# Signs and router steps at written places, exact parts tile by tile, weight sums at the seam, and the last stores on other queues, in an attention and gated feed-forward kernel

## The chip, the cores and the metric

The kernel runs on one core of one Trainium2 chip. TensorE (PE) multiplies matrices into PSUM banks; VectorE (DVE), ScalarE (ACT) and GpSimd (POOL) do elementwise work; SyncE (SP) here only issues transfers, and ACT's and POOL's instruction queues can issue them too. All engines run side by side and wait for each other by semaphores. The metric is the time of one execution on the device in microseconds (us), less being better. The kernel before took 1203.75 us (median of 3 runs, 1203.04 to 1204.23).

## The reference

Everything is float32. The input is 4 sequences of 512 rows of 1024 numbers. With `_layernorm`, a causal attention with 16 heads of 64 and rotary positions, and a feed-forward part whose weight matrix counts only by its signs:

```python
q = (xn @ Wq).reshape(b, s, 16, 64)          # k, v likewise; q and k are rotated
logits = jnp.where(causal, q @ k.T, -1e9) / jnp.sqrt(64)
s = (softmax(logits) @ v).reshape(b, s, 1024) @ Wo

routing = softmax(xn @ gate_w.T)             # 8 experts
in_scale, out_scale = routing @ in_channel_scale, routing @ out_channel_scale
g = silu(xn * in_scale @ sign(weight).T * out_scale + bias)

out = x + s * g
```

## The kernel before

**Stages.** The projections to Q, K and V and the attention run first, as 16 groups: 4 batches `b` by 4 groups `g` of two head pairs. Group k computes its own projections while it does the attention of group k - 1. Then comes a seam, in which the attention of the last group is done beside the first feed-forward products, and then eight pairs of row tiles (`pairs`, index `q`) with feed-forward product, output projection and the final gating.

**Order.** Only TensorE's instructions run in the order in which the program writes them (`manual_schedule(engines={PE})`). The queues of the other engines, SP's transfers too, are ordered by a planner at compile time, in which what is written earlier goes first among what is ready.

**A group.** `project(b, g)` is a generator. It makes three projections (m = 0, 1, 2 for Q, K, V), each as seven products of half-size blocks in the manner of Strassen and Winograd, with sums `S1..S4` of weights (`form_w`, L249) and `T1..T4` of inputs (`form_x`, L261) on VectorE. It yields after every matmul (Q, K) or every second one (V), 28 times a projection, 84 times a group. Each projection takes four PSUM banks one after another from the pool `ring` (4 banks): its products 1 and 2 (L329 to L334), 7 and 6, 5 and 4, and 3. The third bank is freed by the addition at L356, the fourth by the one after product 3 (recorded at L327). The pool is shared with the transposed probabilities (`ptp`), the attention output (`pv`), the transposes of x and the router's three small banks.

The other work of a group is a list of `pieces`. `attention_pieces` makes 16 of them: five transposes of the first unit's probabilities, `scores_1` with `values`, five transposes of the second unit, `scores_3` with `values`, an empty place, `scores_02`, two empty places. `interleave` deals the 84 steps evenly among the pieces. A first transpose (L457) of the next group needs the probabilities of `scores_02`: mask (L402), maximum (L406), exponential on ScalarE (L409), reciprocal (L417) and a multiplication on GpSimd (L419), first for the block of 384 columns, then for that of 128.

**Extras.** In the first group of a batch (`g == 0`) six pieces are spread evenly between the others: the load of two tiles of the weight matrix, `router(b, 0)` (64 matmuls of x with the gate weights `gw`, L495), `make_sign` of the first tile (four VectorE instructions, L573 and L574), `router(b, 1)` (a transpose and the softmax over the experts on VectorE, L506 to L532), `make_sign` of the second tile, and `router(b, 2)` (a transpose, a copy, four small stores). With 22 pieces they stand at places 3, 7, 11, 15, 19 and 21, `scores_3` at 14 and `scores_02` at 17. The very first group has no attention; there the same extras and the load and split of the two scale tables (`split_scales`, L557 to L564) are its only pieces, nine of them. Eight of its 84 steps have been run before it starts.

**The seam.** `load_xn` brings back the normalized rows of pairs 0 and 1 into one tile. `in_scales` multiplies them by the routed scales. `split(q)` makes a part `hi` that float32r holds exactly (ScalarE, L632) and the rest `lo` (VectorE, L633), for both row tiles of a pair into one buffer (pool `hl`, one deep). `ffn` multiplies both by the signs (L821), 16 steps a pair, and VectorE takes the result out of its ring bank (L831). `sum_wo` (L813) makes the sums t1 to t4 of the output weights, four instructions each: t1 and t3 beside pair 0's products, t2 beside pair 1's, t4 written in `project_out(0)`. t1 lies in the place of pair 0's rows, t2 in that of pair 1's; the gate values `Z` of pair 1 lie in a tile shared with t4. `out_scales(1)` (L642, copied by ScalarE at L652) uses the banks of the scores.

**The end.** `project_out(q)` makes the output projection by seven products (L933), `finish` adds and gates them, and GpSimd's queue stores the rows. For the last pair product 3 comes last, with two VectorE steps (L982, L983) and the last store on SP (L984) behind it; the rows of the other tile are stored from GpSimd's queue (L973).

## Time and profile before

| what | value |
|---|---|
| median of the runs shown | 1203.75 us (1203.04 to 1204.23) |
| profiled execution, its own time | 1201.24 us |
| its span | 1199.5 us |
| mean granted TensorE clock | 0.996 of full speed |
| TensorE instructions on the chain that ended last | 89% of the span |
| VectorE on that chain | 7% |
| bytes read and written in HBM | 95.45 MB and 25.43 MB, 101 GB/s over the span |

The span is one execution from the first to the last recorded instruction; the profiled execution's own time holds 1.7 us more. A row of a timeline reads: start, duration, engine, line of the program, operation, output<-input, shape, how many were merged, and in brackets how long the engine had been idle and what ended that. A row of windows reads: the stretch, its length, busy time of PE, PEld (weight loads), DVE, ACT and POOL with the number of instructions in brackets, the granted clock of TensorE, the busy share of the DMA engines and what they moved in GB/s. A float32 matmul is recorded as two instructions, one in float32r as one.

In windows of 20 us over the whole span TensorE is busy for the full 20 us in most of them. The others are 0 to 40, 80 to 100, 260 to 280, 460 to 480, 680 to 700, 840 to 860, 880 to 900 and 1180 to 1200 us.

### The profile page before, as it was taken

What the parts mean: (1) busy time and instruction counts of PE and PEld (TensorE: products, weight loads), DVE (VectorE), ACT (ScalarE), POOL (GpSimd) and SP (SyncE); (2) the same over time, 40 slices, a digit from 0 to 9 for tenths busy, and PEclk for the clock granted to TensorE, in tenths of its full rate; (3) what the DMA queues carried; (4) which work ended last, traced back from release to release, by engine and by line L of the source; (5) the groups of instructions that cost most, each with busy time, mean ns of one, the idle gap of its engine ahead of it and who ended that gap; (6) DMA issues with size and microseconds to landing.
All of it is one profiled execution on the core that took longest, in us unless ns stands there. A gap on an engine that the chain in (4) does not pass through costs nothing.

```text
span 1199.5 us, 17805 instructions
## 1 busy us (share of the span) xinstructions
PE 1170.3 (98%) x6696; PEld 888.1 (74%) x6696; DVE 773.5 (64%) x1395; ACT 492.6 (41%) x1134; POOL 536.3 (45%) x596
## 2 busy tenths in 40 slices
PE   6999999999999999999999999999999999999997
PEld 5988888877878887887888878887764456645663
DVE  6878677776767678576767866666864533453342
ACT  2453655344464644356464534445432121222120
POOL 0464536353443635343353534255355445544543
PEclk9999999999999999999999999999999999999999
DMA  8414323332143232223325212210503523432320
GB/s 299 143 54 136 119 84 109 99 99 80 44 127 111 80 118 94 71 73 115 114 89 185 66 60 80 80 49 19 207 15 138 194 76 105 145 112 68 106 70 36
DMA packets 59814, 122.04 MB, mean 102 GB/s; under 512 B 5200, under 2 KB 40528, under 8 KB 53584
## 3 DMA queue, kind: packets, MB, share of 16 engines
q1 hardware_dynamic: 55008, 111.98, 28.7%
q0 software_dynamic: 4720, 8.92, 2.1%
q8 instruction: 53, 0.87, 0.3%
q14 instruction: 33, 0.27, 0.1%
HBM read 95.45 MB, written 25.43 MB: 101 GB/s over the span
## 4 chain that ended last, share of the span: by engine, by line
PE 89%; DVE 7%; ACT 2%; issue 1%; POOL 0%; DMA 0%; ACTq 0%; DVEq 0%
PE pj L300 32%; PE wo L933 16%; PE pj L308 13%; PE ff L821 9%; PE pv L473 6%; PE sc L391 6%; PE ptp L457 6%; DVE nmx L406 2%; ACT p L409 1%; PE xtp L205 1%; DVE sc L402 1%; PE lg L495 1%; DVE rot L271 1%; DVE S L249 0%; DVE lo L633 0%
## 5 line engine op out<-in xcount | busy, mean ns | idle before, releaser
L419 POOL TENSOR_SCALAR p<-p,rs 128x128 f32<-128x128 f32 (+3 forms) x256 | 169.3, 674 | 204.6 <-DVE rs L417 204.6
L409 ACT ACTIVATE p<-sc,nmx 128x128 f32<-128x128 f32 (+3 forms) x256 | 132.5, 523 | 154.2 <-DVE nmx L406 146.1
L300 PE MATMUL pj<-T,S 128*128 128x256 f32 x768 | 182.3, 380 | 2.2 <-DVE T L261 2.2
L300 PEld LDWEIGHTS pj<-T,S 128*128 128x128 f32 x768 | 140.1, 190 | 20.6 <-DVE T L261 3.0
L300 PE MATMUL pj<-X,w 128*128 128x256 f32 x512 | 126.0, 388 | 6.5 <-DVE v L356 6.4
L355 POOL TENSOR_TENSOR part<-part,part 128x256 f32<-128x256 f32 x48 | 37.2, 774 | 197.8 <-ACT part L354 193.8
L272 POOL TENSOR_TENSOR sw<-sw,sin_sb 128x512 f32<-128x512 f32 x64 | 84.5, 1320 | 85.1 <-ACT sw L270 81.7
L300 PEld LDWEIGHTS pj<-X,w 128*128 128x128 f32 x512 | 94.5, 194 | 19.1 <-DVE v L356 7.1
L406 DVE TENSOR_REDUCE nmx<-sc 128x2 f32<-128x512 f32 (+3 forms) x128 | 103.5, 819 | 2.5
L821 PE MATMUL ff<-sg,hi 128*128 128x512 f32 x256 | 103.5, 404 | 0.0
L463 ACT COPY pT<-ptp 128x512 f32<-128x512 f32 x96 | 56.0, 586 | 114.0 <-PE ptp L457 113.4
L249 DVE TENSOR_TENSOR S<-w 128x512 f32<-128x512 f32 x96 | 81.7, 853 | 31.3 <-PE pj L300 27.6
L821 PE MATMUL ff<-sg,lo 128*128 128x512 f32 x256 | 99.9, 390 | 0.0
L457 PE MATMUL ptp<-ident,p 128*128 128x128 f32 x640 | 95.9, 274 | 2.9 <-DVE z_t L831 1.1
L308 PE MATMUL pj<-S,T 128*128 128x128 f32 x768 | 92.4, 277 | 2.3 <-DVE S L249 2.3
L457 PEld LDWEIGHTS ptp<-ident,p 128*128 128x128 f32 x640 | 79.1, 142 | 18.7 <-DVE z_t L831 1.6
L269 ACT ACTIVATE sw<-c 32x512 f32<-32x512 f32 x128 | 80.4, 628 | 27.6 <-DVE c L327 25.7
L308 PEld LDWEIGHTS pj<-S,T 128*128 128x128 f32 x768 | 88.2, 192 | 4.4 <-DVE S L249 2.5
L273 POOL TENSOR_TENSOR rot<-rot,sw 128x512 f32<-128x512 f32 x64 | 84.6, 1322 | 4.8
L391 PE MATMUL sc<-rot,rot 64*128 64x384 f32 (+3 forms) x512 | 82.0, 449 | 0.0
L270 ACT ACTIVATE sw<-c 32x512 f32<-32x512 f32 x128 | 80.4, 628 | 1.8
L473 PE MATMUL pv<-pT,v 128*64 128x256 f32 (+3 forms) x512 | 76.0, 439 | 0.0
(137 smaller groups left out, 1990.7 us busy)
## 6 DMA issues: line engine op xcount, KB each, us to landing
w<-in_wqkv SPq DMA_DIRECT2D x48, 1024.0 KB
x<-in_x SPq DMA_DIRECT2D x16, 512.0 KB
xn_d<-X SPq DMA_DIRECT2D x16, 512.0 KB
at_d<-at SPq DMA_DIRECT2D x32, 256.0 KB
xp<-xn_d SPq DMA_DIRECT2D x16, 512.0 KB
ap<-at_d SPq DMA_DIRECT2D x16, 512.0 KB
xr<-in_x SPq DMA_DIRECT2D x16, 512.0 KB
wb<-in_wb SPq DMA_DIRECT2D x8, 512.0 KB
```

What stands on the lines that cost most here:

```text
L272: nc.gpsimd.tensor_tensor(sw, sw, sin_sb, op=ALU.mult)
L273: nc.gpsimd.tensor_tensor(rot, rot, sw, op=ALU.add)
L300: nc.tensor.matmul(ps, lhsT=wq[:, k, :], rhs=xq[:, k, :], start=(k == 0), stop=(k == 3))
L308: nc.tensor.matmul(ps[:, j * P : (j + 1) * P], lhsT=xq[:, k, j * P : (j + 1) * P], rhs=wq[:, k, :], start=(k == 0), stop=(k == 3),)
L391: nc.tensor.matmul(ps[:, h, :], lhsT=Q[u][r : r + D, i * P : (i + 1) * P], rhs=K[u][r : r + D, : (i + 1) * P], start=True, stop=True,)
L406: nc.vector.tensor_reduce(nmx, ps, AX.X, ALU.max, negate=True)
L409: nc.scalar.activation(pt[:, h, :], ps[:, h, :], AF.Exp, bias=nmx[:, h : h + 1], accum_out=ssum[:, h : h + 1],)
L419: nc.gpsimd.tensor_scalar(pt[:, h, :], pt[:, h, :], rs[:, h : h + 1], 1.0, op0=ALU.mult, op1=ALU.mult,)
L457: nc.tensor.transpose(tp[:, k, :], probs(u, i)[:, h, j * P : (j + 1) * P], ident)
L473: nc.tensor.matmul(pv[r : r + D, j * P :], lhsT=V[u][:, j, r : r + D], rhs=PT[u][:, n, o : o + (TPB - j) * P], start=(j == 0), stop=(j == ...
L821: nc.tensor.matmul(acc, lhsT=part[q][:, i, c, :], rhs=sg[4 * k + c // 2][:, (c % 2) * HALF : (c % 2 + 1) * HALF], start=(c == 0 and part i ...
L933: nc.tensor.matmul(ps, lhsT=lhs[:, k, :], rhs=rhs[:, k, :], start=(k == 0), stop=(k == 3))
```

## The change

Five edits. (1) In the first group of a batch the six extras stand at places that are written out: loads first, the first sign tile behind the fourth transpose, router step 0 behind `scores_1`, the second sign tile directly after it, router steps 1 and 2 between the second unit's transposes. The very first group starts with router step 0, loads the scales and splits them earlier in its list, and ends with two empty places. (2) `split` works on one row tile, with the pool `hl` two deep and each buffer half as large; at the seam the four halves are written apart from each other. (3) All 16 instructions of `sum_wo` are written beside pair 0's products; t2 moves to the shared tile, and pair 1's `Z` to the place of pair 1's rows. (4) `out_scales(1)` is written behind `scores_02` and uses the ring's banks; ten instead of nine steps of pair 1's products follow it before the last transposes. (5) In the last pair the rows of the second tile are stored from ScalarE's queue, and product 3 is computed and stored in two halves of 256 columns, the first from ScalarE's queue, the second from SP's.

```diff
-    def split(q):
-
-        HI[q] = hl.tile([P, 2, NC, P], F32R, tag="hi", name=f"hi_{q}")
-        LO[q] = hl.tile([P, 2, NC, P], F32R, tag="lo", name=f"lo_{q}")
-        for i in range(2):
-            for c in range(0, NC, 4):
-                xs, hi, lo = (v[:, i, c : c + 4, :] for v in (XP[q], HI[q], LO[q]))
-                nc.scalar.copy(hi, xs)
-                nc.vector.tensor_tensor(lo, xs, hi.bitcast(F32), op=ALU.subtract)
+    def split(q, i):
+
+        HI[q, i] = hl.tile([P, NC, P], F32R, tag="hi", name=f"hi_{q}_{i}")
+        LO[q, i] = hl.tile([P, NC, P], F32R, tag="lo", name=f"lo_{q}_{i}")
+        for c in range(0, NC, 4):
+            xs, hi, lo = (v[:, c : c + 4, :] for v in (XP[q][:, i], HI[q, i], LO[q, i]))
+            nc.scalar.copy(hi, xs)
+            nc.vector.tensor_tensor(lo, xs, hi.bitcast(F32), op=ALU.subtract)
...
         if g == 0:
-            extra = [
-                lambda: (load_sign(2 * b), load_sign(2 * b + 1)),
-                lambda: router(b, 0),
-                lambda: make_sign(2 * b),
-                lambda: router(b, 1),
-                lambda: make_sign(2 * b + 1),
-                lambda: router(b, 2),
-            ]
-            if b == 0:
-                extra[5:5] = [lambda: (load_scales(in_scale), load_scales(out_scale))]
-                extra += [lambda: split_scales(isc), lambda: split_scales(osc)]
+            loads = lambda: (load_sign(2 * b), load_sign(2 * b + 1))
+            signs = [lambda n=n: make_sign(2 * b + n) for n in range(2)]
+            routing = [lambda n=n: router(b, n) for n in range(3)]
+            if k == 0:
+                pieces = [
+                    routing[0],
+                    loads,
+                    routing[1],
+                    *signs,
+                    lambda: (load_scales(in_scale), load_scales(out_scale)),
+                    routing[2],
+                    lambda: split_scales(isc),
+                    lambda: split_scales(osc),
+                    lambda: None,
+                    lambda: None,
+                ]
+            else:
+
+                for at, piece in (
+                    (0, loads),
+                    (5, signs[0]),
+                    (8, routing[0]),
+                    (9, signs[1]),
+                    (12, routing[1]),
+                    (15, routing[2]),
+                ):
+                    pieces.insert(at, piece)
...
-    hl = pool(name="hl", bufs=1)
+    hl = pool(name="hl", bufs=2)
...
-    rest = xp.tile([P, 2, 4, HALF], F32, tag="X", name="z1_t4")
-    t4 = rest[:, 1]
-    z_place[1] = [rest[:, 0, 2 * i : 2 * i + 2, :].rearrange("p c n -> p (c n)") for i in range(2)]
+    rest = xp.tile([P, 2, 4, HALF], F32, tag="X", name="t2_t4")
+    t2, t4 = rest[:, 0], rest[:, 1]
+    z_place[1] = [XP[1][:, i].rearrange("p c q -> p (c q)") for i in range(2)]
...
-    sums = iter([(n, c) for n in (1, 3) for c in range(4)])
+    sums = iter([(n, c) for n in (1, 3, 2, 4) for c in range(4)])
...
-    split(0)
     for n in range(5):
         transpose_p(w, n)
+    split(0, 0)
     scores_1(units)
+    split(0, 1)
     values(w)
     gates = gated(0)
...
     dense(gates, 6)
-    out_scales(1, score_banks)
+
+    split(1, 0)
     dense(gates, 4)
     for _ in gates:
         pass
-    split(1)
+    split(1, 1)
     scores_02(units)
+    out_scales(1)
     gates = gated(1)
-    sums = iter([(2, c) for c in range(4)])
-    dense(gates, 9)
+    dense(gates, 10)
...
-        if q == 0:
-            for c in range(4):
-                sum_wo(4, c)
...
-        nc.gpsimd.dma_start(out=out[rows[1], :], in_=Z[q, 1])
+        (nc.scalar if last else nc.gpsimd).dma_start(out=out[rows[1], :], in_=Z[q, 1])
...
-        ps = product(3, SA[q, 4], b22)
         if last:
-            nc.vector.tensor_tensor(z, ps, z, op=ALU.mult)
-            nc.vector.tensor_tensor(z, z, u2, op=ALU.add)
-            nc.sync.dma_start(out=out[rows[0], HALF:], in_=z)
+
+            for n in range(2):
+                cols = slice(n * TH, (n + 1) * TH)
+                ps = ps_wo.tile([P, TH], F32, tag="wo", name=f"wo_{q}_3_{n}")
+                for k in range(4):
+                    nc.tensor.matmul(
+                        ps,
+                        lhsT=SA[q, 4][:, k, :],
+                        rhs=b22[:, k, cols],
+                        start=(k == 0),
+                        stop=(k == 3),
+                    )
+                nc.vector.tensor_tensor(z[:, cols], ps, z[:, cols], op=ALU.mult)
+                nc.vector.tensor_tensor(z[:, cols], z[:, cols], u2[:, cols], op=ALU.add)
+                queue = (nc.scalar, nc.sync)[n]
+                queue.dma_start(out=out[rows[0], HALF + n * TH : HALF + (n + 1) * TH], in_=z[:, cols])
         else:
+            ps = product(3, SA[q, 4], b22)
             finish(0, 1, ps, u2)
```

More of the change, by code (lines that the diff above doesn't have):

```diff
@@ L796, in attn_gated_ffn_kernel @@
     b11, b12, b21, b22 = (quarter[fk] for fk in ((0, 0), (0, 1), (1, 0), (1, 1)))
-    t1, t2 = (
-        XP[q].rearrange("p i c q -> p (i c q)").rearrange("p (c n) -> p c n", n=HALF) for q in range(2)
-    )
+    t1 = XP[0].rearrange("p i c q -> p (i c q)").rearrange("p (c n) -> p c n", n=HALF)
     t3 = b12
-    rest = xp.tile([P, 2, 4, HALF], F32, tag="X", name="z1_t4")
-    t4 = rest[:, 1]
-    z_place[1] = [rest[:, 0, 2 * i : 2 * i + 2, :].rearrange("p c n -> p (c n)") for i in range(2)]
+    rest = xp.tile([P, 2, 4, HALF], F32, tag="X", name="t2_t4")
+    t2, t4 = rest[:, 0], rest[:, 1]
+    z_place[1] = [XP[1][:, i].rearrange("p c q -> p (c q)") for i in range(2)]
     def sum_wo(n, c):
@@ L822, in ffn @@
                     acc,
-                    lhsT=part[q][:, i, c, :],
+                    lhsT=part[q, i][:, c, :],
                     rhs=sg[4 * k + c // 2][:, (c % 2) * HALF : (c % 2 + 1) * HALF],
@@ L1003, in attn_gated_ffn_kernel @@
                 lambda: None,
-                lambda: (in_scales(q + 1), split(q + 1)),
+                lambda: (in_scales(q + 1), split(q + 1, 0), split(q + 1, 1)),
                 lambda: out_scales(q + 1),
```

## The prediction

> **What bounds the kernel now.** I read the page's first table first, then TensorE's list of waits, then the timelines around each wait, the granted clock there, and the end of the span.
>
> ```profile
> span 1199.5 us, 17805 instructions
> PE 1170.3 (98%) x6696; PEld 888.1 (74%) x6696; DVE 773.5 (64%) x1395; ACT 492.6 (41%) x1134; POOL 536.3 (45%) x596
> ```
>
> TensorE is the bound, and the change leaves its arithmetic as it is. Only its idle time can be won or lost: 1199.5 - 1170.3 = 29.2 us, and what a slow clock adds behind an idle stretch. TensorE's waits (total, times, longest) say where it lies:
>
> ```profile
> PE xtp L205 <- DVE x L193: 8.9, 2, 8.7
> PE pj L300 <- DVE v L356: 6.4, 3, 2.2
> PE pj L308 <- DVE S L249: 2.3, 1, 2.3
> PE pj L300 <- DVE T L261: 2.2, 2, 1.6
> PE ptp L457 <- DVE z_t L831: 1.1, 1, 1.1
> PE ptp L457 <- POOL p L419: 0.8, 2, 0.6
> PE ptp L457 <- DVE pT L461: 0.5, 1, 0.5
> PE ptp L457 <- DVE v L327: 0.3, 1, 0.3
> ```
>
> The first row is the start (x has to land); the change doesn't touch it. The second is the end of the groups (1,0), (2,0) and (3,0), at 261.2, 475.8 and 688.8 us. VectorE's timeline there:
>
> ```profile
> 258.57 0.51 DVE L573 TENSOR_SCALAR sg<-wb 128x512 fp32r<-128x512 f32 x1
> ...
> 261.28 0.73 DVE L574 SCALAR_TENSOR_TENSOR sg<-wb,sg 128x512 fp32r<-128x512 f32 x1
> ...
> 262.62 0.67 DVE L356 TENSOR_TENSOR v<-pj,part 128x512 f32<-128x512 f32 x1
> ```
>
> The second sign tile of the batch (four instructions, 2.6 us) runs among the last softmax steps, ahead of the addition that frees the accumulator bank TensorE wants. The router's last transpose, written at the group's last place, holds a fourth bank. Each wait is 2.2, 2.2 and 2.0 us, and the clock (third figure from the end of a row of windows) can fall behind it:
>
> ```profile
> 480.00:481.00 1.00, 1.00 (x8) 0.85 (x7) 0.00 (x0) 0.00 (x0) 0.00 (x0) 1.00 0.14 33
> 692.80:693.80 1.00, 1.00 (x4) 0.82 (x3) 0.00 (x0) 0.00 (x0) 0.00 (x0) 0.50 0.14 33
> ```
>
> After 478 us it stays at 1.00. After 690.8 us it is 0.50: ten matmuls take 3.9 us, where elsewhere ten take 2.16, so 1.7 more; after 263.3 likewise 1.7. **These three places cost 2.2+1.7, 2.2+0.1 and 2.0+1.7 = 9.9 us.** The Trainium skill (TensorE: Matmul & The Clock Gate, Part 1) lets the clock fall only after an idle window of about 3.4 us; by that the three would cost 6.4 us and the sum below would be 3.5 us smaller. Rows of 0.50 behind 2.2 us of idling decide.
>
> **The change, part by part.**
>
> *Signs and router at written places.* The instructions are the same; only their places change. A group has 84 fill steps of 0.44 us (two recorded matmuls of L300 at 0.216 us, or four of L308 at 0.111), dealt to its pieces. With 22 pieces, piece n comes after 84n/22 steps. Before, the second signs stood at step 73 and the last router step at 81; after, at 35 and 58. So VectorE meets the group's end as in an ordinary group, where TensorE doesn't wait at all. The price: everything put in front pushes the scores back. The last scores (blocks 0 and 2) go from step 65 to 73, an ordinary group has them at 69. The next group's first transpose needs their probabilities 11 steps = 4.9 us after the scores end. The ordinary group's chain:
>
> ```profile
> 307.13 2.00 PE L391 MATMUL sc<-rot,rot 64*128 64x384 f32 x16
> ...
> 313.38 1.15 POOL L419 TENSOR_SCALAR p<-p,rs 128x128 f32<-128x128 f32 x2 [0.88 <-DVE rs L417]
> ...
> 315.86 0.60 PE L457 MATMUL ptp<-ident,p 128*128 128x128 f32 x4
> ```
>
> Scores end at 309.1, the first probabilities (half of the 1.15) are ready at 313.9: 4.8 us; in the groups at 359.6 and 735.7 us 4.5 and 4.7. So the chain just fits, and its cover is gone: each 0.1 us that VectorE is late is 0.1 us of TensorE. I leave 0.5 us per group for that: **gain 9.9 - 1.5 = 8.4 us**, bounds 9.9 (nothing left) and 0.4 (waits of 2 us come back with the same clock). The middle gets fuller. Between steps 35 and 58 TensorE has 11.5 us of work (23 steps, three banks of transposes). VectorE's regular work there is 7.1 us by its rows (four sums S and two copies at 0.69, four additions at 0.42, L356 0.69, one rotary 0.65); the signs add 2.2 to 4.2 (at 229.4 us the four took 4.2 beside GpSimd) and the router's softmax 3.4: 12.7 to 14.7, a backlog of 1 to 3 us, which the 3.5 us before the next scores, holding 1.4 us of such work, mostly clears. The sign loads are two 512 KB issues on SP; the first was issued at 178.2 us, the second at 206.7, just before the group that they are written in, so both lie hidden. Behind them on SP stand weight loads used more than 20 us later.
>
> *First group.* Its router matmuls come first instead of after ten steps: 64 matmuls, 25.08 to 27.03 us, 1.95 us. TensorE is free at 18.1 and waits 1.55 us and 0.61 us for VectorE's T sums (row four); the matmuls fit into these 2.2 us if X (last copy ends 18.4) and the gate weights are there. The latter's small packets pass the DMA queues between 16 and 18 us. Landed at 18.4, all of 1.95 is won; at 20.8, nothing; later costs its lateness. **I take 1.5**, near the early end, where the packets are. The scale loads come 8 steps = 3.5 us sooner. The split of out_scale (L562 to L564, 1.22 + 0.84 + 1.30 = 3.4 us on VectorE, with ScalarE's 1.06 before it) now stands at 86.5 to 91.3 us straight ahead of the sum S that TensorE awaits for 2.3 us (row three). Moved 3.5 us up it is clear of it: 2.3; if it meets a softmax instead, -1. **I take 1.4.** SP's load of x (held from about 70 to 91.3 us for this buffer) and the two weight loads queued behind it go sooner too; nobody waits for them here.
>
> *The seam (847 to 906 us).* Splits by tile and a two-deep buffer: the four transposed copies no longer stand behind the exact parts (row seven, 0.5), and pair 1's first half is split under pair 0's products. Eight weight sums (0.68 us each, t2 and t4) go from 881 to 893 us, where VectorE is full, to 866 to 876.6 us, where it is busy 3.6 of 10.6 us; with two lo parts that is 6.9 us into 7.0 free. That cover is exactly used up, but nothing there is awaited for 9 us. Rows five and six (1.1 + 0.8) go with the sums. Row eight stays. New: out_scales(1) takes the four ring banks behind the last scores, so the next product waits for ScalarE's first copy out of them (0.52 us by L652): 0.5 us, or up to 2 if exps of 0.69 us stand before it. The bank wait now stands before pair 1's whole product; ScalarE's exps queue behind its four copies, 2.1 us, with 9 us to spare. **Gain 0.5 + 1.9 - 0.5 = 1.9**, bounds 2.4 and 0.4. t4 leaves project_out(0), where it delayed nothing: 0.
>
> *The end.* TensorE stops at 1193.12.
>
> ```profile
> 1193.86 0.59 POOL L973 DMA_DIRECT2D out<-z_t  x1 [0.30 <-POOL z_t L945]
> ...
> 1194.66 0.34 SPq L984 DMA_DIRECT2D out<-z_t  x1
> ...
> 1196.75:1197.00 0.25, 0.00 (x0) 0.00 (x0) 0.00 (x0) 0.00 (x0) 0.00 (x0) 0.50 0.84 320
> ```
>
> Two DVE steps (0.70, 0.69) follow, then 768 KB leave in one piece from 1195.0 to 1197.05 at some 400 GB/s (last figure of the window), then 2.45 us to the close. In halves, TensorE's work is the same (16 x 0.216 = 8 x 0.43). The last DVE steps are 128x256: 0.42 each by L327, done at 1194.1, 0.6 sooner. The 512 KB row goes from ScalarE's queue, which has been idle since 1186.9. No row shows an issue there; between SP's (0.34 us; data 0.8 us after the issue at 1178.9) and POOL's (0.59; 1.1 after 1193.86) I take SP's, because ScalarE's queue, like SP's, holds nothing else then. It is still held by GpSimd's last addition, to 1193.56; behind it in ScalarE's queue waits only the first half's store. Data from 1194.4, the same 2.05 us for the same bytes: end 1196.45, **gain 0.6**, bounds 0.2 (POOL's rows) and 1.0. The Trainium skill (DMA: Bandwidth & Descriptors, Bandwidth) speaks against cutting: transfers should be 1 MiB, and 64 KB take 0.95 us, an estimated 0.76 above their bytes; added here that would turn the 0.6 into a loss of 0.2. The rows show two transfers sharing 400 GB/s without a gap.
>
> **Sum.** 8.4 + 1.5 + 1.4 + 1.9 + 0.6 = 13.8 us. Span 1199.5 to 1185.7; the profiled execution took 1201.2, of which 1.7 lie around the span: 1187.4. The median of the runs shown, 1203.75, is 2.5 above it, so **1190.0**. All upper bounds, 9.9 + 2.0 + 2.3 + 2.4 + 1.0 = 17.6, give 1186.2. The likeliest case's own range is 1186 to 1193.
>
> **Rivals.**
> - *The scores come too near the group's end.* The wait moves from L356 to the multiplication by the reciprocal sum (L419). For it: 4.9 us of room against 4.5 to 4.8 needed; in group (1,0), with VectorE loaded, the chain took 6.5 (scores end 251.9, multiplication 258.3). Against: that load is what moves away. Waits of 2 us three times, with 3.5 us of slow clock, leave 0.4 of the first term: 13.8 - 8.0 = 5.8, so 1198.0.
> - *The opening gives nothing.* Gate weights late and the scale split lands on another awaited sum: -1.5 and -1.4 - 1.0, so 13.8 - 3.9 = 9.9, 1193.9. For it: VectorE is 81% busy from 60 to 80 us, where the split would go.
> - *Slower: VectorE can't hold the middle of the three groups.* Signs, router and ordinary work between steps 35 and 58, all at their longest (4.2 + 6.0 as the router's chain ran from 246.6 to 252.6 + 7.1 x 1.3 beside GpSimd = 19.4) against 11.5 us: backlog 7.9. The four ring banks cover some 2 us; the rest, 5.9 us a group, TensorE waits at a transpose for L356 of the middle projection. 13.8 - 17.7 = -3.9, so 1207.7; slower than before from 6.6 us of backlog. Against: the same router chain did run beside the heavier last scores with a loss of 2.2.
> - *The places don't hold.* Only TensorE's order is written; the other queues are ordered by a planner, which ran the first sign load at 178.2, far ahead of its place. If it puts the signs back among the late scores, the first term goes and with it most else that hangs on VectorE: about 1203.
>
> **How the numbers follow.** Likeliest case 0.60; scores too near 0.14; opening 0.13; middle 0.09; places 0.04. Forecast 1190.0. The range 1186 to 1198.5 takes in the first three, 0.87. Within 0.2% (about what a measurement of this kernel can tell from no change) is 1201.3 to 1206.2: only the last case, 0.04. Faster 0.87, slower 0.09.
>
> **What would show it.** Right: no TensorE wait on L356, none on S in the second group; the clock at 1.00 through all group ends; router matmuls at 18 to 20 us; no TensorE wait on L831 or L419 at the seam; the last data gone some 0.6 us sooner after TensorE stops. Wrong: waits on L419 at the first transpose of groups (1,1), (2,1), (3,1); on ScalarE's copy of os at the seam beyond 1 us; a wait in mid-group; router matmuls waiting for gw.

## The result, and the profile after

The changed kernel takes 1204.23 us (median of 20 runs, 1203.16 to 1205.49), the kernel before 1202.28 us on the same chip (median of 20, 1199.77 to 1204.23). The ratio is 1.0016, 95% interval 1.001 to 1.0023: very slightly slower. Forecast were 1190.0 us and a range from 1186 to 1198.5.

The page of the changed kernel's profile begins like this (span; busy time and share of each engine). Lines are those of the kernel that ran: L641, L651, L834 and L844 of the changed kernel are L642, L652, L821 and L831 of the kernel before, and in the experiments they can lie a few lines off.

```profile
span 1203.7 us, 17814 instructions
PE 1170.4 (97%) x6704; PEld 891.0 (74%) x6704; DVE 764.6 (64%) x1397; ACT 492.9 (41%) x1134; POOL 533.3 (44%) x595
```

TensorE's work is what it was (1170.3 before). Its list of waits (total, times, longest) is not:

```profile
PE pj L300 <- DVE S L249: 10.4, 1, 10.4
PE xtp L205 <- DVE x L193: 9.0, 2, 8.7
PE ff L834 <- ACT xp L651: 5.6, 1, 5.6
PE ptp L457 <- POOL p L419: 1.5, 3, 0.5
PE lg L495 <- DMA gw<-in_gate_wT: 0.7, 1, 0.7
PE pj L308 <- DVE part L327: 0.3, 1, 0.3
PE ptp L457 <- DVE v L327: 0.3, 1, 0.3
PE pj L300 <- ACT X L211: 0.2, 1, 0.2
```

All waits that the change was forecast to remove are gone: L356 (6.4), T (2.2), L831 (1.1), pT (0.5), S on L308 (2.3), and those on L419 at the seam (0.8). The row on L419 that is left is three waits of 0.5 us behind the first groups of batches 2 to 4, as forecast. In the place of the others stand two single waits, rows one and three. To see what each stage gained or lost, take four points that both kernels have and subtract their times in the two profiled executions:

| stage, from one point to the next | before | after | difference |
|---|---|---|---|
| start to the first transpose of the second batch's x (L205) | 107.69 | 117.28 | +9.6 |
| from there to the first feed-forward product | 746.90 | 737.67 | -9.2 |
| from there to the first output product | 51.17 | 55.99 | +4.8 |
| from there to the end of TensorE's last product | 287.35 | 287.50 | +0.1 |
| from there to the end of the span | 6.39 | 5.26 | -1.1 |
| span | 1199.5 | 1203.7 | +4.2 |

So the small change of the whole is made of large ones: the middle won 9.2 us and the end 1.1, the opening lost 9.6 and the seam 4.8. (The spans differ by 4.2 us and the medians by 1.95: the profiled execution of the kernel before, 1201.24 us, was 1.0 quicker than its median, that of the changed kernel, 1205.41 us, 1.2 slower.)

**The opening.** TensorE's timeline in the second group (start, duration, engine, line, what, and in brackets the idle time before and what ended it):

```profile
70.41 3.62 PE L300 MATMUL pj<-X,w 128*128 128x256 f32 x16
84.44 5.49 PE L300 MATMUL pj<-T,S 128*128 128x256 f32 x12 [10.42 <-DVE S L249]
```

VectorE's timeline over the same wait:

```profile
73.25 1.29 DVE L271 SCALAR_TENSOR_TENSOR rot<-c,cos_sb 128x512 f32<-128x512 f32 x2
79.46 1.33 DVE L562 TENSOR_TENSOR scales<-scales,osc 128x1024 f32<-128x1024 f32 x1 [4.92 <-ACT osc L561]
80.83 1.64 DVE L563 TENSOR_SCALAR scales<-scales,is_high 128x1024 f32<-128x1024 f32 x1
82.50 1.28 DVE L564 SCALAR_TENSOR_TENSOR osc<-osc,is_high,scales 128x1024 fp32r<-128x1024 f32 x1
83.70 1.28 DVE L249 TENSOR_TENSOR S<-w 128x512 f32<-128x512 f32 x2
```

And the end of a run of eight rotary copies on ScalarE, which began at 73.25:

```profile
77.73 0.63 ACT L270 ACTIVATE sw<-c 32x512 f32<-32x512 f32 x1
78.38 1.04 ACT L561 CAST osc<-scales 128x1024 fp32r<-128x1024 f32 x1
```

Read it from the bottom. The cast of out_scale waits for its turn behind the eight copies. The split of out_scale waits for the cast, and VectorE stands idle for 4.92 us. The sum S, which TensorE has wanted since 74.0, waits behind the split. No operand of S is missing: its weights were requested at 47.4 us, and the DMA engines, at 401 GB/s from 50 to 51 us, are down to 15 GB/s from 52 to 53 and to 0 in the microsecond after it, ahead of the next transfer. Its buffers are free too: the last products that read the sums of the projection before began at 68.68 us and took 1.89. S is only the next instruction in a queue whose head is stuck. Here a statement of the Trainium skill fits (PSUM — Partial Sum Buffer, Engine vs sequencer instructions): "ScalarE/VectorE/GpSimdE queues are strict FIFO." The rows agree: 4.92 us idle, with ready work behind the head.

The wait is followed by a slow clock, the third figure from the end of a row of windows:

```profile
80.00:85.00 5.00, 0.56 (x1) 0.50 (x2) 4.91 (x5) 0.00 (x0) 5.00 (x7) 0.50 0.20 33
85.00:90.00 5.00, 5.00 (x14) 3.52 (x12) 2.41 (x4) 0.00 (x0) 1.32 (x3) 0.50 1.00 335
```

Twelve matmuls of this kind take 5.49 us there and 2.86 a little later, so 2.6 more.

In the kernel before, the four sums of this projection stood ahead of the split (VectorE ran them from 62.8 to 74.6 us), and the cast came ahead of the next rotary copies:

```profile
85.25 1.06 ACT L561 CAST osc<-scales 128x1024 fp32r<-128x1024 f32 x1
...
88.76 0.63 ACT L269 ACTIVATE sw<-c 32x512 f32<-32x512 f32 x1 [1.36 <-DVE c L327]
```

**The seam.** In the kernel before, the four os products went to banks of the scores, and ScalarE emptied these at once (TensorE, then ScalarE):

```profile
872.45 0.51 PE L642 MATMUL os<-osc,rt 32*128 32x512 f32 x4
872.99 2.06 ACT L652 COPY z_t<-os 128x512 f32<-128x512 f32 x4 [3.97 <-PE os L642]
```

TensorE, VectorE and ScalarE of the changed kernel, in this order:

```profile
878.37 0.89 PE L641 MATMUL os<-osc,rt 32*128 32x512 f32 x4
884.90 0.80 PE L834 MATMUL ff<-sg,hi 128*128 128x512 f32 x1 [5.64 <-ACT xp L651]
```

```profile
878.63 3.05 DVE L632 TENSOR_TENSOR lo<-xp,hi 128x512 fp32r<-128x512 f32 x2
881.61 0.42 DVE L402 TENSOR_TENSOR sc<-sc,mask 128x256 f32<-128x256 f32 x1
882.06 0.96 DVE L406 TENSOR_REDUCE nmx<-sc 128x2 f32<-128x768 f32 x1
```

```profile
883.14 0.58 ACT L409 ACTIVATE p<-sc,nmx 128x384 f32<-128x384 f32 x1 [5.64 <-DVE nmx L406]
...
884.27 1.56 ACT L651 COPY xp<-os 128x512 f32<-128x512 f32 x3
```

The four os products fill all four ring banks at 879. ScalarE could empty them at once, and is idle; but the head of its queue is an exponential, which waits for VectorE's maximum, which stands behind the exact part `lo` (3.05 us for two). It is the same figure as in the opening: an idle engine, and ready work behind a head that waits. Behind it the clock is at 0.50 until about 889.

### The profile page after: what moved, and what is told of

Its sections match the earlier page's. It is cut to its first block, busy times and chain, and to the rows that moved or that the text cites. A ratio compares the mean times of both kernels' runs of the same rounds, so it can differ in the third digit from the quotient of the medians.

```text
span 1203.7 us, 17814 instructions
## 1 busy us (share of the span) xinstructions
PE 1170.4 (97%) x6704; PEld 891.0 (74%) x6704; DVE 764.6 (64%) x1397; ACT 492.9 (41%) x1134; POOL 533.3 (44%) x595
## 4 chain that ended last, share of the span: by engine, by line
PE 91%; DVE 4%; DMA 1%; ACT 1%; issue 0%; POOL 0%; SPq 0%; ACTq 0%; DVEq 0%
PE pj L300 31%; PE wo L948 16%; PE pj L308 15%; PE ff L834 9%; PE pv L473 6%; PE sc L391 6%; PE ptp L457 6%; DMA gw<-in_gate_wT 1%; DVE nmx L406 1%; PE xtp L205 1%; ACT p L409 1%; PE lg L495 1%; DVE S L249 0%; DVE lo L632 0%; DMA x<-in_x 0%
## 5 line engine op out<-in xcount | busy, mean ns | idle before, releaser
L419 POOL TENSOR_SCALAR p<-p,rs 128x128 f32<-128x128 f32 (+3 forms) x256 | 166.6, 664 | 188.7 <-DVE rs L417 188.7
L300 PE MATMUL pj<-T,S 128*128 128x256 f32 x768 | 185.3, 384 | 10.4 <-DVE S L249 10.4
L300 PE MATMUL pj<-X,w 128*128 128x256 f32 x512 | 122.5, 381 | 0.2 <-ACT X L211 0.2
L834 PE MATMUL ff<-sg,hi 128*128 128x512 f32 x256 | 104.5, 408 | 5.6 <-ACT xp L651 5.6
L834 PE MATMUL ff<-sg,lo 128*128 128x512 f32 x256 | 101.0, 395 | 0.0
L308 PE MATMUL pj<-S,T 128*128 128x128 f32 x768 | 92.9, 277 | 0.0
L308 PEld LDWEIGHTS pj<-S,T 128*128 128x128 f32 x768 | 88.3, 192 | 2.2 <-issue 0.5
```

Source lines behind the costliest of these rows:

```text
L300: nc.tensor.matmul(ps, lhsT=wq[:, k, :], rhs=xq[:, k, :], start=(k == 0), stop=(k == 3))
L308: nc.tensor.matmul(ps[:, j * P : (j + 1) * P], lhsT=xq[:, k, j * P : (j + 1) * P], rhs=wq[:, k, :], start=(k == 0), stop=(k == 3),)
L419: nc.gpsimd.tensor_scalar(pt[:, h, :], pt[:, h, :], rs[:, h : h + 1], 1.0, op0=ALU.mult, op1=ALU.mult,)
L834: nc.tensor.matmul(acc, lhsT=part[q, i][:, c, :], rhs=sg[4 * k + c // 2][:, (c % 2) * HALF : (c % 2 + 1) * HALF], start=(c == 0 and part i ...
```

## The experiments

Times are medians. Each group of experiments is compared with runs of the kernel before on the same chip (medians 1203.44 us for experiments 1 to 4, 1203.2 for 5 to 8, 1202.95 for 9 to 12, 1203.15 for 13 and 14).

**1. The first group's list as before.**

```diff
-                pieces = [
-                    routing[0],
+                extra = [
                     loads,
+                    routing[0],
+                    signs[0],
                     routing[1],
-                    *signs,
+                    signs[1],
                     lambda: (load_scales(in_scale), load_scales(out_scale)),
                     routing[2],
                     lambda: split_scales(isc),
                     lambda: split_scales(osc),
-                    lambda: None,
-                    lambda: None,
                 ]
```

> The changed kernel with the first group's list as before (nine pieces dealt out, router after the sign loads, no empty pieces); all else as changed. Theory (a queue order set by the new list): the wait of 10.4 us on the sum S in the second group and the slow clock behind it (2.9 us) go, the old wait on S (2.3 us, L308) comes back and the router's early start (1.2 us) is lost: 10.4 + 2.9 - 2.3 - 1.2 = 9.8 us below the changed kernel, about 1194.4, some 8 us below before. Rival (the early part costs little on net, the loss is in the signs' new places): within 2 us of the changed kernel.

Measured 1197.62 us, ratio to before 0.9948 (0.9933 to 0.9963). The wait of 10.4 us is gone, and 2.3 us on L308 <- S is back. The gain over the changed kernel is 6.6 us and not 9.8. Some 2 us of the difference lie behind the old wait: the profile of this run has a clock of 0.83 from 90 to 100 us, that of before 1.00, and it reaches the first transpose of the second batch at 109.71 instead of 107.69 us. Another 1.2 us stay unexplained. The rival falls: the loss of the opening comes with this list.

**2. Copies ahead of the last scores.**

```diff
-    scores_02(units)
     out_scales(1)
+    scores_02(units)
```

> The changed kernel with pair 1's output scales written ahead of the last scores instead of behind them; all else as changed. Theory (ScalarE's copies that free the ring banks stand in its queue behind exponentials that wait for VectorE): the seam's wait of 5.6 us on the copy L651 falls below 0.5 and the slow clock behind it (some 2 us) goes: 7 to 7.6 us below the changed kernel, about 1197. Rival (the four banks taken at once are the cause, whatever the order): the copies of the second tile still wait for VectorE's exact part, and at least 3 us of the wait stays.

Measured 1199.04 us, 0.9963 (0.9948 to 0.9978), 5.2 below the changed kernel. The wait of 5.6 us becomes another one:

```profile
PE os L641 <- DVE z L844: 1.2, 1, 1.2
```

Now the third os product waits until VectorE has emptied a bank of the last product. The seam takes 50.2 us, against 56.0 in the changed kernel and 51.2 before, and the clock stays at 1.00. So the order of the copies makes most of the wait, but the need for four banks leaves something, and the time is 2 us above the 1197 expected.

**3. The cast on VectorE.**

```diff
-        nc.scalar.copy(dst, v)
+        nc.vector.tensor_copy(dst, v)
```

> The changed kernel with the cast in the scale split (L561) on VectorE instead of ScalarE, so VectorE waits for no other engine there. Theory (VectorE stands idle for 4.9 us before the split because the cast is behind eight rotary copies on ScalarE): VectorE casts from 74.5 us (some 1.1 us), the split follows (1.3 + 0.8 + 1.3) and the sum S starts at 79.0 instead of 83.7: TensorE's wait falls from 10.4 to about 5.7, the clock behind it stays slow, time 4 to 5 us below the changed kernel. Rival (S waits for its weights, held on SyncE's queue behind the loads of x, or the scales land late): within 1 us of the changed kernel.

Measured 1203.59 us, 0.6 below the changed kernel's 1204.23; ratio to before 1.0005 (0.9996 to 1.0014). In the profile the wait on S falls from 10.4 to 8.6, the place at 107 us is reached 1.9 us sooner (115.41 against 117.28). My 4 to 5 us failed. VectorE's timeline tells why:

```profile
75.22 0.69 DVE L561 CAST osc<-scales 128x1024 fp32r<-128x1024 f32 x1
75.94 1.23 DVE L562 TENSOR_TENSOR scales<-scales,osc 128x1024 f32<-128x1024 f32 x1
77.21 1.64 DVE L563 TENSOR_SCALAR scales<-scales,is_high 128x1024 f32<-128x1024 f32 x1
78.88 2.17 DVE L564 SCALAR_TENSOR_TENSOR osc<-osc,is_high,scales 128x1024 fp32r<-128x1024 f32 x1
80.97 3.42 DVE L249 TENSOR_TENSOR S<-w 128x512 f32<-128x512 f32 x2
```

The idle time is gone, but the split itself still stands ahead of S and takes 5.8 us, and the two sums take 1.71 us each where others take 0.69. GpSimd's rotary steps run beside them from 76.6 to 83.8. So the late cast is only part of the cause: without its 4.92 us of idling, 8.6 us of the wait stay, in which VectorE runs the split and then the sums, both slower than elsewhere.

**4. The signs alone, on the kernel before.** For the first groups of batches 2 to 4:

```diff
+                for at, piece in (
+                    (0, loads),
+                    (5, signs[0]),
+                    (8, routing[0]),
+                    (9, signs[1]),
+                    (12, routing[1]),
+                    (15, routing[2]),
+                ):
+                    pieces.insert(at, piece)
```

> The kernel before with only the signs and the router of the second to fourth batch at their written places; first group, seam and end as before. Theory (the prediction's first term): no wait on L356 in the three groups, 0.5 us on L419 at each next group: 8.4 us below before, about 1194. Rival (part of the 9.9 us comes back as waits elsewhere in these groups, so the loss of the whole change lies here): less than 4 us below before.

Measured 1193.09 us, 0.9919 (0.9902 to 0.9935): 10.3 below before. No wait on L356 is left, and in the list of waits there is

```profile
PE ptp L457 <- POOL p L419: 2.3, 5, 0.6
```

of which 0.8 in two waits belong to the seam, as before; 1.5 in three are the predicted 0.5 per group. In the profiled executions the stretch from 107 us to the seam is 738.5 against 746.9 us: 8.4. The median's 10.3 is more, because the kernel before mostly runs longer than in its profiled execution: its runs lie near 1199.7, 1201.3 and 1203.5 us, with a mean granted clock of 0.997, 0.996 and 0.994 to 0.995. How often the clock falls behind waits of some 2 us would give such steps; that was not looked at run by run.

**5. The scale loads behind the router.** On experiment 2, two pieces exchanged:

```diff
-                    lambda: (load_scales(in_scale), load_scales(out_scale)),
                     routing[2],
+                    lambda: (load_scales(in_scale), load_scales(out_scale)),
```

> The kernel of the second experiment (copies ahead of the last scores) with two pieces of the first group's list exchanged: the scale loads are written behind the router's last step, so the weight load w(1,1) goes out on SyncE's queue after 3 of the 32 scale loads instead of behind all of them; nothing else is changed. Theory (the late place of that weight load in the written order makes the planner put the four sums S behind the split of out_scale in VectorE's queue): the four sums stand ahead of the split again, the wait of 10.4 us goes and with it 2.9 us of slow clock: 13 us below the second experiment (1199.0), about 1186. Rival 1 (the split's 4 us on VectorE are too early by themselves and meet another awaited step): at least 3 us of waiting stays, about 1189 or more. Rival 2 (the weights arrive late): no change, 1199.

Measured 1200.5 us, 0.9979 (0.9967 to 0.999): no gain over experiment 2. The order came as my theory had it, the gain did not; rival 1 was right. The weight load did go ahead (45.3 us), the four sums did stand ahead of the split and TensorE didn't wait for them. But now the sums of the next projection stand behind the split:

```profile
PE pj L308 <- DVE S L249: 8.9, 1, 8.9
```

and the cast has the next six rotary copies ahead of it:

```profile
91.63 0.63 ACT L270 ACTIVATE sw<-c 32x512 f32<-32x512 f32 x1
92.28 1.04 ACT L561 CAST osc<-scales 128x1024 fp32r<-128x1024 f32 x1
```

**6. The split in the next group.** On experiment 2, the loads left where the change put them:

```diff
-                    lambda: split_scales(osc),
+                    lambda: None,
...
+            if k == 1:
+                pieces.insert(11, lambda: split_scales(osc))
```

> The kernel of the second experiment with the split of out_scale written in the second group, after its twelfth piece, and the scale loads left where the change put them. Theory (the place of the loads decides, not that of the split): VectorE's order has the split ahead of the four sums S as before, and the wait on S stays at 9 us or more: 1199 within 1.5 us. Rival (the split was moved too far forward): the wait goes, about 1186.

Measured 1197.85 us, 0.9962 (0.9949 to 0.9976); the wait on S is 8.4 us, somewhat under the 9 expected. VectorE's compiled order has the split ahead of the same four sums as before the edit. Taken with 5: the written place of the split did not move it, that of the loads did; and at both places in the second group where it landed, a set of sums stood behind it.

**7. The end alone, on the kernel before.** The change's edit 5, and nothing else:

```diff
-        nc.gpsimd.dma_start(out=out[rows[1], :], in_=Z[q, 1])
+        (nc.scalar if last else nc.gpsimd).dma_start(out=out[rows[1], :], in_=Z[q, 1])
...
+            for n in range(2):
+                cols = slice(n * TH, (n + 1) * TH)
```

> The kernel before with only the end changed (last outputs by other queues, last product in halves). From the trace of the changed kernel: TensorE's last product ends 5.3 us before the span does, against 6.4 us before, so 1.1 us below before. The prediction's term: 0.6, bounds 0.2 and 1.0. Rival (the smaller transfers cost as much as the earlier start brings): within 0.2 us of before.

Measured 1200.1 us, 0.9978 (0.9969 to 0.9986). In the profiled execution TensorE's last product ends 5.23 us before the span does, before 6.39: 1.16 us. The medians differ by 3.1, which is more than the end can give: the runs of either kernel lie in three steps (here near 1198.5, 1200.1 and 1202.4 us), and each step is about 1.1 below that of before. One of 11 runs lies in the slowest step here, 15 of 24 before; why so few is not known. The rival falls.

**8. The seam alone, on the kernel before.** The change's edits 2 to 4:

```diff
+    split(1, 0)
     dense(gates, 4)
...
+    split(1, 1)
     scores_02(units)
+    out_scales(1)
     gates = gated(1)
-    dense(gates, 9)
+    dense(gates, 10)
```

> The kernel before with only the seam changed (exact parts tile by tile, weight sums early, pair 1's output scales by the ring banks behind the last scores). Theory: the waits on L831, L419 and L461 (2.4 us) go and a wait of 5.6 us on the copy with 2 us of slow clock comes: 5.2 us above before. Rival (the seam's wait needs the shift that the other parts bring): within 2 us of before.

Measured 1207.7 us, 1.0041 (1.0028 to 1.0054): 4.5 above before. The wait of 5.6 us is there in full, without any of the other parts; the rival falls.

**9. out_scale in the last batch.** On experiment 2:

```diff
-                    lambda: (load_scales(in_scale), load_scales(out_scale)),
+                    lambda: load_scales(in_scale),
...
-                    lambda: split_scales(osc),
+                    lambda: None,
+                    lambda: None,
...
+            if g == 1:
+                pieces.insert(0, lambda: load_scales(out_scale))
+                pieces.insert(12, lambda: split_scales(osc))
```

(the last three lines in the branch of the last batch).

> The kernel of the second experiment (copies ahead of the last scores) with the load and the split of out_scale written in the second group of the last batch, where nothing else is split and no next batch is normalized; the split of in_scale stays in the first group's list. Theory, mended by the fifth and sixth experiments (TensorE loses 9 to 10 us wherever the split of out_scale stands in VectorE's queue ahead of the sums S while its cast stands behind the rotary copies on ScalarE): nothing stands ahead of the sums in the second group, no wait on S above 0.5 us there, no slow clock: 13 us below the second experiment (1199.0), 1186 to 1187. Rival 1 (VectorE in the first two groups is too full whatever stands there): waits on S of 3 us and more stay, 1190 or above. Rival 2 (the split costs as much in the last batch): a new wait of that size there, about 1196.

Measured 1188.68 us, 0.9888 (0.9873 to 0.9903). TensorE waits for no S at all, and reaches the first transpose of the second batch at 103.92 us, 12.9 before experiment 2 (116.81), as the mended theory has it. Neither rival is seen: the split costs nothing visible in the last batch. The total is 2 us short of the expectation, all of it at the seam, which took 53.4 us here and 50.2 in experiment 2. The wait there is the same, 1.3 us on L641; but behind it the clock fell. TensorE's windows in this kernel:

```profile
864.00:865.00 1.00, 0.16 (x1) 0.16 (x1) 1.00 (x3) 1.00 (x3) 0.13 (x1) 1.00 0.00 0
...
867.00:868.00 1.00, 1.00 (x8) 0.70 (x6) 1.00 (x1) 0.36 (x1) 1.00 (x2) 0.50 0.08 16
```

**10. Four weight sums later.** On experiment 9, the last four steps of pair 0 carry no sums:

```diff
     split(1, 0)
-    dense(gates, 4)
     for _ in gates:
         pass
```

> The ninth experiment's kernel, in which the last four weight sums are no longer written among pair 0's last products but among pair 1's. Theory (in the second experiment TensorE waits 1.2 us for a bank that VectorE frees, L844, behind three weight sums of 2.7 us): the wait goes, 1.2 us below the ninth experiment. Rival (the sums meet VectorE's softmax and bring back a wait of before at the following transposes): no gain or a loss of up to 2 us.

Measured 1188.34 us, 0.9885 (0.987 to 0.9899): not told apart from experiment 9. The wait on L641 is still 1.2 us. But the edit did not change VectorE's order: three sums still stand ahead of the step that frees the bank,

```profile
862.60 2.71 DVE L830 TENSOR_TENSOR t_t<-wo,t_t 128x512 f32<-128x512 f32 x3
865.23 1.27 DVE L848 TENSOR_TENSOR z<-ff,z 128x512 f32<-128x512 f32 x2
```

as in experiment 9 (at 861.48 and 864.11). So the theory was not put to the test, and whether the sums hold the bank stays open.

**11. Signs and end, on the kernel before.** The edits of experiments 4 and 7 together.

> The kernel before with the two parts that gained by themselves: signs and router of the later batches at written places, and the end. First group and seam as before. If the parts are independent: 10.3 + 1.1 below before, about 1192.

Measured 1193.77 us, 0.9927 (0.9912 to 0.9941), no better than the signs alone (1193.09). Its profile shows the end's gain (5.3 us behind TensorE's last product) and that of the signs (738.5 us from the second batch's first transpose to the seam). But it reaches that transpose 1.6 us later than experiment 4 (109.54 against 107.95), with the same list of waits: behind the 2.3 us on S the clock is 0.83 from 90 to 100 us here, 1.00 there. With four runs each this pair neither shows nor excludes that the medians differ by the end's 1.1 us.

**12. The first group alone, on the kernel before.** The list of eleven pieces that experiment 1 took out, put into the kernel before.

> The kernel before with only the first group's list changed. Theory (the list costs by itself what it costs in the whole change): waits of 10.4 us on S in the second group with 2.9 us of slow clock, against 2.3 us and the 1.2 us won at the start: 8 to 10 us above before, 1211 to 1213. Rival (it costs this only together with the signs' new places): within 3 us of before.

Measured 1211.03 us, 1.0068 (1.0051 to 1.0085): 8.1 above before. The wait of 10.4 us on S is there without the other parts; the rival falls.

**13. Output scales in two halves, the first ahead of the scores.** On experiment 9, the first tile's two os products ahead of the last scores, the second tile's two after five steps of pair 1's products (`part` says which of the four products are made; two of them take two ring banks):

```diff
-    out_scales(1)
+    out_scales(1, part=(0, 1))
     scores_02(units)
     gates = gated(1)
-    dense(gates, 10)
+    dense(gates, 5)
+    out_scales(1, part=(2, 3))
+    dense(gates, 5)
```

> The ninth experiment's kernel with pair 1's output scales in two halves: the first tile's two banks ahead of the last scores, the second tile's two banks after five steps of pair 1's products, so that never more than two ring banks wait for a copy. Theory (what is left at the seam comes from four banks being asked for at once: a wait of 1.3 us for a bank that VectorE frees late, and in the ninth experiment's profile 3.2 us more while the clock is at 0.50): no wait at the seam but the 0.3 us on L327, clock at 1.00 from 840 to 900 us, 1.3 us below the ninth experiment (1188.7) and up to 4.5 us, so 1184.2 to 1187.4. Rival (the halves come back as a wait of the same size, for the second tile's copies behind the exponentials): 1188 or more.

Measured 1185.39 us, 0.9859 (0.9842 to 0.9875), the best version found: 17.8 below before, 18.8 below the change. Its page and its whole list of waits:

```profile
span 1183.4 us, 17798 instructions
PE 1165.8 (99%) x6704; PEld 887.3 (75%) x6704; DVE 762.2 (64%) x1397; ACT 492.8 (42%) x1134; POOL 536.0 (45%) x595
```

```profile
PE xtp L205 <- DVE x L193: 9.0, 2, 8.7
PE ptp L457 <- POOL p L419: 1.5, 3, 0.5
PE pj L308 <- DVE part L327: 0.9, 1, 0.9
PE ptp L457 <- DVE v L327: 0.3, 1, 0.3
PE lg L495 <- ACT X L211: 0.2, 1, 0.2
PE ff L841 <- DVE xp L851: 0.2, 1, 0.2
```

The seam takes 49.0 us, with the clock at 1.00 throughout. PE's busy time is 3.1 us less than in experiment 9 (1168.9): that is the slow clock, since matmuls at half clock count as busy.

**14. The same halves, behind the scores.** On the changed kernel; the copies stay behind the exponentials.

> The changed kernel with only this made otherwise: pair 1's output scales in the same two halves, the first behind the last scores, where the change put all four. The copies still stand behind the exponentials. Theory of the banks (the seam's wait of 5.6 us needs four banks taken at once and late copies together): the next product finds a free bank, the wait falls to 1.5 us or less and the slow clock goes: 6 to 7 us below the changed kernel, about 1198. Theory of the queue alone (as the second experiment was read): the copies are as late as before and TensorE waits at least 3 us for one of them, about 1201 or more.

Measured 1199.78 us, 0.9973 (0.9964 to 0.9983), 4.5 below the changed kernel. ScalarE's first copies come as late as in the change, at 884.59; TensorE meanwhile works on and waits only at the second half:

```profile
885.22 0.98 PE L644 MATMUL os<-osc,rt 32*128 32x512 f32 x2 [1.31 <-ACT xp L654]
```

The theory of the banks holds in the wait: late copies cost 1.3 us with two banks taken and 5.6 with four, and the clock stays at 1.00. The seam takes 50.4 us, 5.6 less than in the changed kernel; the gain of 4.5 in the medians is less than the 6 to 7 expected. So the wait needs both, all four banks and copies behind a waiting head; either remedy removes most of it, and both together, in experiment 13, all.

## Why the prediction was wrong, point by point

- **Signs and router at written places: right.** Forecast +8.4, with 0.5 us left per group on L419. The profiles show exactly these three waits, 1.5 us in total, and a stretch shorter by 9.2 in the changed kernel and 8.4 with the signs alone. The tight chain of scores held, and neither the rival of late scores nor that of a crowded middle came about.
- **First group's router first: right, a little small.** Forecast +1.5. The router's products run at 18.89 us after 0.7 us of waiting for gw, the waits on T are gone, and the next group's first scores come 1.2 us sooner (55.0 against 56.3).
- **The scale split moved 3.5 us up: wrong, the main failure.** The step was: "Moved 3.5 us up it is clear of it: 2.3; if it meets a softmax instead, -1. I take 1.4." The 2.3 did go. But the split moved by more than its written place: it began at 79.46 us instead of 86.47, 7.0 sooner, and so ahead of the sums of the projection before. And the bound of -1 priced the split as a piece of work that somebody waits for once. It is a chain over two queues: the cast needs ScalarE, the split holds VectorE until it has come, and the sums behind it hold TensorE. It cost 10.4 us and 2.6 of slow clock, and experiment 9, which takes the split away from there, gets 12.9 us back. Of the loads, the working followed only those of x and the weights behind them ("nobody waits for them here"), not what the scale loads themselves were moved past: the weight load w(1,1), which on SP's queue went from 42.05 to 47.41 us. Its data still came in time, but in VectorE's compiled order the four sums that need it went behind the split; experiment 5, which exchanges the loads again, brings them back ahead of it. What the profile of before did show was the price: a cast behind eight copies of 0.63 us, and the split of 3.4 us after it, are 5.0 + 1.06 + 3.4 = 9.5 us if a set of sums lands behind them. That should have been the lower bound.
- **The seam: half right.** Forecast were +2.4 for the old waits, and they went. The failed step is the price of the new wait: "0.5 us, or up to 2 if exps of 0.69 us stand before it". I priced the work of the exponentials, not the time until they may start: 5.64 us in which ScalarE idles for a maximum that stands behind the `lo` parts on VectorE. I had seen that VectorE's cover there was "exactly used up" and concluded that nothing there is awaited for 9 us; the copies were. With the slow clock the seam lost 4.8 us instead of winning 1.9. A wait on this copy beyond 1 us stood among the prediction's signs of being wrong.
- **The end: right in sign, small in size.** Forecast 0.6, bounds 0.2 and 1.0; measured 1.1. The data starts 1.5 us behind TensorE's last product instead of 1.9, and 1.7 us instead of 2.45 lie between the last data and the close of the span. The shorter close was not in the working, and its cause wasn't tried; nor was the halving tried without the other queues. The loss of 0.2 that the prediction estimated for smaller transfers did not come.
- **The sum.** Without the two waits the parts are worth what was forecast and more: experiment 13, which keeps all five edits and only places out_scale's table and pair 1's output scales otherwise, is 17.8 us below before (16.1 between the profiled spans), against 13.8 predicted. The rival of the opening named the right place, a split that lands on another awaited sum, but priced it at 1.0 us; what I had left out is a rival that ends on the slower side by a blocked queue. My slower rival was about VectorE's amount of work, and the runs show no wait that came from that amount in the middle of the three groups.

## What to carry to other kernels

When a step is moved, ask for every in-order queue it passes through which instruction will stand at its head, what that one waits for, and which ready work lies behind it; price the wait by the time until the head can start, not by the work ahead of it. A chain that hops over two engines (a cast on one, the rest on another) can block both, so put it where neither has awaited work behind it, even far from where it is needed. Taking the last free bank turned late copies into a wait of TensorE of 5.6 us here; taking two of four left it something to do, and 1.3.

## What the runs showed that was not expected

- The clock can fall behind a short wait, and not each time. The same wait of 2.3 us on S leaves it at 1.00 from 90 to 100 us before and in experiments 4 and 7, and at a mean of 0.83 in experiments 1, 8 and 11. A wait of 1.2 to 1.3 us at the seam left it at 1.00 in experiments 2 and 14, brought it to 0.50 for some 3 us in experiments 5, 6 and 10, and for some 6 us in experiment 9, which cost 3.2 us there. The Trainium skill (TensorE: Matmul & The Clock Gate, Part 1) lets the clock fall after an idle window of about 3.4 us, and calls the window free-running. The second would fit different outcomes of one wait. The first does not fit waits of 1.2 to 2.3 us, and the measurement decides. Around the wait at the seam stand products that use only 32 or 64 of 128 rows (os, scores); whether these count as idle was not tried.
- VectorE's sums of two tiles took 1.71 us instead of 0.69 beside GpSimd's rotary steps (experiment 3), and the multiplication by is_high 1.64 us instead of the 0.75 at 63.54 us in the changed kernel. That GpSimd is the cause was not tried.
- Executions of one kernel differ in steps of about 2 us that go with the mean granted clock (before: near 1199.7, 1201.3 and 1203.5 us). The four runs of experiment 13, which behind its start has no wait above 0.9 us, show no such steps: they lie between 1185.15 and 1186.13.
